# Keeping the first batch's embedding sums in DRAM for the second batch

## The chip, the cores and the metric

The kernel runs on one core of a Trainium2 chip. The metric is the device time of one execution in microseconds, the median of three runs. The profile is one more execution, taken by the hardware profiler.

The engines are named as in the profile: PE is the matrix engine (PEld its weight loads), DVE the vector engine, ACT the scalar engine, POOL the GpSimd engine, and SP the engine that issues most of the DMA transfers. A name with a q behind it (SPq, POOLq) is the engine's sequencer, which issues transfers.

## The reference

Two layers of attention work on a tensor of 2 batches, 512 channels and 64 x 32 = 2048 positions. The change concerns layer 0 alone. Its queries and keys are projections of the channels together with a position embedding of 64 rows, 32 of which depend on the row h of the position and 32 on its column w:

```python
emb = get_embeddings(B, H, W, FREQ_DIM, TIME_DIM, hidden_states.dtype)
qk_hs = jnp.concatenate([hidden_states, emb], axis=1)
qk_hs = qk_hs.reshape(B, -1, S).transpose(0, 2, 1)
q = qk_hs @ Wq
k = qk_hs @ Wk
v = v_hs @ Wv
...
scores = jnp.einsum('bhqd,bhkd->bhqk', q, k) * scale
attn = jax.nn.softmax(scores, axis=-1)
o = jnp.einsum('bhqk,bhkd->bhqd', attn, v)
...
return o + hidden_states
```

`get_embeddings` broadcasts the same embedding over the batches. The embedding's share of q and of k is thus the same for both batches. Layer 1 (a layer norm, Nystroem attention with landmarks, a residual and a feed-forward map) follows, and the change does not touch it.

## The kernel before, in words

All numbers are float32. Layer 0 goes through eight pairs of heads, four of batch 0 and then four of batch 1; pair (b, hp) is the two heads hp of batch b, 128 channels. The class `Heads0` (line 857) holds what a pair needs before its attention: q and k of 128 x 2048, and v. For q and for k this is

- the embedding's sum (`embedded`, lines 877 to 890). The embedding is kept as 64 rows by 64 + 32 columns, one column for each h and each w. A matmul (line 880) gives the projection of these 96 columns in a PSUM bank `fp`; DVE copies it to `ft` (line 882); POOL adds the part of h and the part of w, both broadcast, to `e`, 128 x 2048 (line 884). The pool `wpool0` has one buffer for each name, so `e` has one buffer, which q and k of all pairs share in turn;
- four projections, one for each block of 512 positions (lines 892 to 899): four matmuls into a PSUM bank `pp`, and a DVE add of the bank and the block of `e` into q or k.

The banks `fp`, `pp`, `vp`, `yp`, `mean`, `var` and `rs` all come from `bank()` (line 730), which has two buffers in turn.

The first pair does all this at the start of the kernel, with nothing beside it. SP issues the first loads there, about 7 MB, in this order: the first 128 columns of the query weights, the first block of x, the first 128 columns of the key weights, the other three blocks of x, the value weights, and the rest of the query and key weights.

Each further pair is prepared while the pair before it runs its attention. `attention0` (line 1045) goes through 4 blocks of queries (t) by 16 chunks of keys (c) in groups of two steps: the scores of two steps (PE, line 1057), the exps (ACT, line 1065), the sums of the exps (DVE, line 1075), and the values of the group before (PE, line 1087). After a group it may take units of work from a list of generators, the fillers. How many are due follows from a count: `due = n_filler * (i + GROUP) // len(steps)`, and `advance` takes up to three when two or more are due. A generator that yields `GAP` has nothing to do in this turn: the call goes on to the next generator, and the gap counts as no unit. `Heads0.N_UNITS` (line 860) is the count for one pair: 5 units for q, 5 for k, 4 for v and the bound.

The units of a pair are, for q: the embedding's matmul, copy and sum as a unit of its own, a gap, and four projections. Then the same for k, then four units of v. In pair (1,0) the order is another: its attention also has the residual projection and the norm of batch 0 as fillers (`finish0_units`, line 1017), and takes at least one unit after each group; the pair prepared there, (1,1), does k and v first, and q last, once the residual projection has used the q of batch 0 (`ready`, line 923). What is left of the units is done after the last group without attention beside it. In that stretch the norm's steps are (lines 971 to 1013): the sum over the four chunks of channels (DVE, 974 and 975), the mean (PE, 978), the difference (DVE, 979), the squares (ACT, 982 and 985) and their sum (DVE, 987 and 988), the variance (PE, 991), its root (ACT, 993), the reciprocal (DVE, 1008), the scaling (POOL 1010, DVE 1011), and the store of `xh` (POOL's queue, 1012). The block `xr` is loaded on SP's queue (1021).

After each block of queries, `sums` (line 1097) adds up the exps over the partitions (PE, `rs`), takes the reciprocal (DVE, 1102), spreads it by eight small transfers on SP's queue (`rinv`, line 789), and scales o on POOL (1105).

PE, DVE, ACT and POOL run their instructions in the order of the program. The order on SP's queue is set by a scheduler when the kernel is built: it puts a transfer as early as what it depends on allows by its own estimate. [...]

Of the kernel before, what the change touches and what calls it, by code (L numbers as in the profile page):

```python
# [10 lines left out]
F32 = mybir.dt.float32  # L11
# [5 lines left out]
P = 128  # L17
B, C, H, W = 2, 512, 64, 32
S = H * W
KC = C // P  # L20
HEADS, D = 8, 64
NPAIR = HEADS // 2
# [637 lines left out]
GAP = object()  # L660
# [3 lines left out]
def fast_path(  # L664
# [35 lines left out]
    nc = tc.nc  # L700
    dram = ctx.enter_context(tc.tile_pool(name="dram1", bufs=1, space=bass.MemoryType.DRAM))
# [12 lines left out]
    wpool0 = only0.enter_context(tc.tile_pool(name="w0", bufs=1))  # L714
# [3 lines left out]
    mT_d = dram.tile([P, KC, C], F32, name="mT_fd")  # L718
    k_d = dram.tile([B, NPAIR, P, S], F32, name="k_fd")
    X_d = dram.tile([B, NPAIR, 2, P, 2, LM], F32, name="X_fd")  # L720
    q_d = dram.tile([B, NPAIR, P, S], F32, name="q_fd")
    o_d = dram.tile([B, NPAIR, P, S], F32, name="o_fd")
    A_d = dram.tile([B, NPAIR, 2, P, 2, LM], F32, name="A_fd")
# [6 lines left out]
    def bank(name):  # L730
        return ps.tile([P, 512], F32, tag="pp", name=name)
# [60 lines left out]
    def advance(gens, n=1):  # L792


        made, i = 0, 0
        while made < n and i < len(gens):
            got = next(gens[i], gens)
            if got is gens:
                gens.pop(i)
            elif got is GAP:  # L800
                i += 1
            else:
                made += 1
        return made
# [5 lines left out]
    def gap(n=1):  # L810
        for _ in range(n):
            yield GAP
# [21 lines left out]
    def load_x(src, b, name, first=0, n=NTB):  # L834
        tiles = []
        for t in range(first, first + n):
            xb = block_of(xpool, "xb", f"{name}_{b}_{t}")
            nc.sync.dma_start(xb, chunked(src[b])[:, :, t * TB : (t + 1) * TB])
            tiles.append(xb)
        return tiles  # L840
# [16 lines left out]
    class Heads0:  # L857


        N_UNITS = 15  # L860

        def __init__(self, b, hp, xbs):
            self.b, self.hp, self.xbs = b, hp, xbs
            self.name = f"f0_{b}_{hp}"

        def begin(self):
            self.cols = slice(self.hp * P, (self.hp + 1) * P)
            self.k = kvpool.tile([P, S], F32, tag="k", name=f"k_{self.name}")
            self.v = kvpool.tile([P, NST, P], F32, tag="v", name=f"v_{self.name}")

        def embedded_and_projected(self, kind):

            cols, xbs = self.cols, self.xbs
            if kind == "q":
                self.q = qopool.tile([P, S], F32, tag="qo", name=f"q_{self.name}")

            def embedded(kind):

                fp = bank(f"fp_{kind}_{self.name}")
                nc.tensor.matmul(fp[:, : H + W], lhsT=we[kind][:, cols], rhs=emb_sb, start=True, stop=True)  # L880
                ft = wpool0.tile([P, H + W], F32, tag="ft", name=f"ft_{kind}_{self.name}")
                nc.vector.tensor_copy(ft, fp[:, : H + W])
                e = wpool0.tile([P, H, W], F32, tag="e", name=f"e_{kind}_{self.name}")
                nc.gpsimd.tensor_tensor(
                    e,
                    ft[:, :H].unsqueeze(2).to_broadcast([P, H, W]),
                    ft[:, H:].unsqueeze(1).to_broadcast([P, H, W]),
                    ALU.add,
                )
                return e.rearrange("p h w -> p (h w)")  # L890

            def project(kind, dst, e, t):
                toks = slice(t * TB, (t + 1) * TB)
                pp = bank(f"pp_{kind}_{self.name}_{t}")
                for k in range(KC):
                    nc.tensor.matmul(  # L896
                        pp, lhsT=w_sb[kind][:, k, cols], rhs=xbs[t][:, k, :], start=k == 0, stop=k == KC - 1
                    )
                nc.vector.tensor_tensor(dst[:, toks], pp, e[:, toks], ALU.add)  # L899

            dst = self.q if kind == "q" else self.k
            e = embedded(kind)
            yield
            yield GAP
            for t in range(NTB):
                project(kind, dst, e, t)
                yield
# [109 lines left out]
    def finish0_units(b, oTs, outs_done):  # L1017
        last = None
        for t in range(NTB):
            xb = block_of(lpool, "xr", f"xr_f0_{b}_{t}")  # L1020
            nc.sync.dma_start(xb, chunked(x[b])[:, :, t * TB : (t + 1) * TB])
            yield from gap()

            for m, _ in enumerate(out0_units(b, t, xb, oTs)):
                if last and m == 0:
                    next(last)
                yield
            if t == NTB - 1:
                outs_done.append(True)
            if last:  # L1030
                yield from gap()
            xn = block_of(lpool, "xn", f"xn_f0_{b}_{t}")
            last = norm0_steps(b, t, xb, xn, xn[:, :2, :])
            next(last)
            yield from gap(2)
            next(last)
            yield
            yield from gap(2)
            next(last)
            yield from gap(2)  # L1040
            next(last)
            yield
        next(last)
# [128 lines left out]
    def load_wo(w, name):  # L1172
        wo_sb = block_of(lpool, "wo", name)
        nc.sync.dma_start(wo_sb, chunked(w))
        return wo_sb
# [13 lines left out]
    def write_bands():  # L1189


        rows = block_of(lpool, "xn", "rows1").rearrange("p k n -> p (k n)")
        rows = rows[:, : HEADS * (BAND + 1)].rearrange("p (h q) -> p h q", h=HEADS)
        nc.vector.memset(rows, 0.0)
        nc.sync.dma_start(rows[:, :, :KER], convr.partition_broadcast(P))
        for h in range(HEADS):
            nc.sync.dma_start(band_d[h].rearrange("(p q) -> p q", q=BAND + 1), rows[:, h, :])
# [498 lines left out]
    oTs, finish, work = [], None, []  # L1696
    for n, (b, hp) in enumerate(todo[:-1]):
        nb, nhp = todo[n + 1]
        if nb != b:
            xbs = load_x(x, nb, "x0")  # L1700
        nxt = Heads0(nb, nhp, xbs)
        n_fill = Heads0.N_UNITS + 2 * len(work)
        if finish is None:
            units = nxt.units(wait=nb - b)
        else:

            units = nxt.units(False, lambda: outs_done)
            work.append(finish)
            n_fill += N_FINISH0
        work.append(units)  # L1710
        attention0(cur, work, n_fill, units, ffn_map if finish is None else None, finish is not None)
        finish = None
        oTs.append(cur.q)
        if n == 3:
            while ffn_map:
                advance(ffn_map)
            wo_sb = load_wo(wo0, "wo_f0")
            write_bands()
        if hp == NPAIR - 1:
            outs_done = []  # L1720
            finish = finish0_units(b, oTs, outs_done)
            oTs = []
        cur = nxt
# [45 lines left out]
    b = B - 1  # L1769
# [300 lines left out]
@with_exitstack  # L2070
def conv_attn_hybrid(
    ctx: ExitStack,
    tc: tile.TileContext,
    x: bass.AP,
    emb: bass.AP,
    freq: bass.AP,
    time: bass.AP,
    wq0: bass.AP,
    wk0: bass.AP,
    wv0: bass.AP,  # L2080
    wo0: bass.AP,
    b0: bass.AP,
    *rest: bass.AP,
):

    nc = tc.nc
    keep = ctx.enter_context(tc.tile_pool(name="keep_f", bufs=1))
    bad = keep.tile([P, 1], F32, name="bad")
    bad_i = keep.tile([P, 1], I32, name="bad_i")
    in_order = {mybir.EngineType.PE, mybir.EngineType.DVE, mybir.EngineType.Activation, mybir.EngineType.Pool}  # L2090
    with tc.manual_schedule(engines=in_order):
        fast_path(tc, x, freq, time, wq0, wk0, wv0, wo0, b0, *rest, bad)
    nc.vector.tensor_copy(bad_i, bad)
    again = nc.values_load(bad_i[:1, :1])
    with tc.If(again > 0):
        general_path(tc, x, emb, wq0, wk0, wv0, wo0, b0, *rest)
# [59 lines left out]
```

## Time and profile before

| | |
|---|---|
| median of three runs | 2775.44 us (2773.93 to 2777.14) |
| profiled execution | 2775.64 us |
| its span in the profile | 2773.8 us |
| mean granted PE clock | 0.993 |
| layer 0's attention ends at about | 1330 us |
| DMA in the whole span | 157.22 MB, mean 57 GB/s |
| L884, POOL sum `e` (16) | 3.6 to 4.6 us each |
| L882, DVE copy `ft` (16) | 0.25 us each |
| L880, PE matmul `fp` (32, two for each sum) | 0.31 us each |

The three rows of L880, L882 and L884 are the work on the embedding's sums, for both batches. A line of the timeline has the start in us, the busy time in us, the engine, the line of the kernel, the operation, and output and inputs; at the end, in brackets, is the idle time of the engine before it and what ended that. Runs of the same instruction are merged, with their count after an x. In the rows by slices, each digit is the busy share of one fortieth of the span in tenths.

### The profile page before, as it was taken

What the parts mean: (1) busy time and instruction counts of PE and PEld (TensorE: products, weight loads), DVE (VectorE), ACT (ScalarE), POOL (GpSimd) and SP (SyncE); (2) the same over time, 40 slices, a digit from 0 to 9 for tenths busy, and PEclk for the clock granted to TensorE, in tenths of its full rate; (3) what the DMA queues carried; (4) which work ended last, traced back from release to release, by engine and by line L of the source; (5) the groups of instructions that cost most, each with busy time, mean ns of one, the idle gap of its engine ahead of it and who ended that gap; (6) DMA issues with size and microseconds to landing.
All of it is one profiled execution on the core that took longest, in us unless ns stands there. A gap on an engine that the chain in (4) does not pass through costs nothing. (4 is left out here: it accounts for less than half of the span.)

```text
span 2773.8 us, 41257 instructions
## 1 busy us (share of the span) xinstructions
PE 2712.4 (98%) x17010; PEld 1365.7 (49%) x17010; DVE 1638.7 (59%) x2076; ACT 905.8 (33%) x1352; POOL 197.2 (7%) x133
## 2 busy tenths in 40 slices
PE   9999999999999999999999999999999999999898
PEld 5343443434343334343344455777677766555334
DVE  3768787774557765747657444544644545556455
ACT  1344343433335244435412223233332323221210
POOL 1101101010001200100002000000000000000000
PEclk9999999999999999999999999999999999999999
DMA  3000000201111200012025532313111202111301
GB/s 115 12 9 9 13 6 7 69 24 50 32 50 54 80 9 7 8 49 64 24 87 186 201 118 92 97 34 115 54 36 58 81 9 90 38 66 31 106 32 47
DMA packets 110358, 157.22 MB, mean 57 GB/s; under 512 B 16065, under 2 KB 67793, under 8 KB 107601
## 3 DMA queue, kind: packets, MB, share of 16 engines
q1 hardware_dynamic: 105664, 137.68, 15.7%
q0 software_dynamic: 4416, 16.79, 1.6%
q8 instruction: 135, 2.21, 0.4%
q14 instruction: 63, 0.51, 0.1%
q10 hardware_dynamic: 80, 0.03, 0.0%
HBM read 82.48 MB, written 55.19 MB: 50 GB/s over the span
## 5 line engine op out<-in xcount | busy, mean ns | idle before, releaser
L1075 DVE TENSOR_TENSOR acc_f<-acc_f,p_f 128x1024 f32<-128x1024 f32 x448 | 589.4, 1316 | 235.6 <-ACT p_f L1065 207.0
L1065 ACT ACTIVATE p_f<-sc_f 128x1024 f32<-128x1024 f32 x512 | 496.4, 1021 | 561.9 <-PE sc_f L1057 550.4
L1057 PE MATMUL sc_f<-q_f,k_f 64*64 64x512 f32 x4096 | 491.7, 595 | 2.4 <-ACT p_f L1065 2.4
L1087 PE MATMUL av_f<-p_f,v_f 64*64 64x512 f32 x4096 | 484.3, 589 | 0.0
L1087 PEld LDWEIGHTS av_f<-p_f,v_f 64*64 64x64 f32 x4096 | 156.5, 133 | 283.0 <-issue 283.0
L1057 PEld LDWEIGHTS sc_f<-q_f,k_f 64*64 64x64 f32 x4096 | 144.8, 133 | 280.9 <-issue 256.0
L1230 PE MATMUL pp<-xh,w 128*128 128x512 f32 x512 | 233.0, 608 | 0.7 <-ACT q L1233 0.7
L1230 PEld LDWEIGHTS pp<-xh,w 128*128 128x128 f32 x512 | 96.5, 194 | 123.2 <-issue 116.0
L1523 PE MATMUL pb<-R 128*128 128x192 f32 (+1 forms) x640 | 151.4, 383 | 1.6 <-DVE M L1536 1.6
L1523 PE MATMUL pa<-M 128*128 128x192 f32 (+1 forms) x640 | 150.6, 380 | 0.0
L941 PEld LDWEIGHTS vp_f<-wv_f,x 128*128 128x128 f32 x1024 | 115.6, 192 | 12.7 <-issue 11.0
L941 PE MATMUL vp<-w,xh 128*128 128x128 f32 x1024 | 120.8, 276 | 0.0
L941 PEld LDWEIGHTS vp<-w,xh 128*128 128x128 f32 x1024 | 117.0, 192 | 7.2 <-issue 4.2
L1523 PEld LDWEIGHTS pb<-R 128*128 128x128 f32 x640 | 107.8, 192 | 25.2 <-DVE M L1536 2.3
L896 PE MATMUL pp_q_f<-x,wq_f 128*128 128x512 f32 x256 | 115.9, 606 | 2.9 <-DMA x<-in_x_dram 1.5
L941 PE MATMUL vp_f<-wv_f,x 128*128 128x128 f32 x1024 | 118.5, 276 | 0.0
L1523 PEld LDWEIGHTS pa<-M 128*128 128x128 f32 x640 | 108.0, 193 | 21.0 <-ACT M L1514 2.5
L956 PE MATMUL yp_g<-o,wo_f 128*128 128x512 f32 x256 | 115.5, 598 | 0.8 <-DVE y_g L1662 0.8
L956 PE MATMUL yp_f<-q_f,wo_f 128*128 128x512 f32 x256 | 114.0, 598 | 2.2 <-issue 1.2
L1673 PE MATMUL fp_g<-xn_g,mT 128*128 128x512 f32 (+1 forms) x264 | 115.7, 589 | 0.0
L896 PE MATMUL pp_k_f<-x,wk_f 128*128 128x512 f32 x256 | 114.1, 599 | 0.4 <-DVE q_f L899 0.4
L1105 POOL TENSOR_TENSOR q_f<-q_f,rinv_f 128x512 f32<-128x512 f32 x32 | 45.9, 1434 | 920.4 <-DMA rinv_f<-acc_f 920.4
(196 smaller groups left out, 2762.0 us busy)
## 6 DMA issues: line engine op xcount, KB each, us to landing
xh<-xh_fd SPq DMA_DIRECT2D x12, 1024.0 KB, 5.4
rinv_f<-acc_f SPq DMA_DIRECT2D x256, 32.0 KB, 1.9
xr_f<-in_x_dram SPq DMA_DIRECT2D x8, 1024.0 KB, 5.2
x_fd<-xr_f POOLq DMA_DIRECT2D x8, 1024.0 KB, 4.6
xh_fd<-xn_f POOLq DMA_DIRECT2D x8, 1024.0 KB, 4.6
k_fd<-k SPq DMA_DIRECT2D x32, 256.0 KB, 2.8
q_fd<-q SPq DMA_DIRECT2D x32, 256.0 KB, 2.9
xb_g<-x_fd SPq DMA_DIRECT2D x32, 256.0 KB, 4.3
```

Source lines behind the costliest of these rows:

```text
L896: nc.tensor.matmul(pp, lhsT=w_sb[kind][:, k, cols], rhs=xbs[t][:, k, :], start=k == 0, stop=k == KC - 1)
L941: nc.tensor.matmul(vp[:, j * P : (j + 1) * P], lhsT=xb[:, k, j * P : (j + 1) * P], rhs=w_of(k), start=k == 0, stop=k == KC - 1,)
L956: nc.tensor.matmul(yp, lhsT=wo_sb[:, k, m * P : (m + 1) * P], rhs=oTs[k][:, toks], start=k == 0, stop=k == NPAIR - 1,)
L1057: nc.tensor.matmul(sc[r * D : (r + 1) * D, h, :], lhsT=hd.k[rows, lo : lo + D], rhs=hd.q[rows, t * TB : (t + 1) * TB], start=True, stop=True,)
L1065: nc.scalar.activation(p, sc, AF.Exp, scale=D**-0.5)
L1075: nc.vector.tensor_tensor(acc, first if c == 1 else acc, p, ALU.add)
L1087: nc.tensor.matmul(av[r][half, :], lhsT=hd.v[keys, c, half], rhs=pp[keys, h, :], start=c == 0, stop=c == NST - 1,)
L1105: nc.gpsimd.tensor_tensor(o, o, rinv, ALU.mult)
L1230: nc.tensor.matmul(pp, lhsT=self.w[j][:, c, :], rhs=xhs[t][:, c, :], start=c == 0, stop=c == KC - 1)
L1523: nc.tensor.matmul(dst, lhsT=lhsT[:, k, t * P : (t + 1) * P], rhs=rhs[:, k, :], start=k == 0, stop=k == 1)
L1673: nc.tensor.matmul(fp[:, cols], lhsT=mT[:, k, m * P : (m + 1) * P], rhs=self.xn[:, k, cols], start=k == 0, stop=k == KC - 1,)
```

## The change

Pairs of batch 0 compute the embedding's sums as before, and store each of them, 1 MB, to a new tensor `e_fd` in DRAM, on SP's queue. Pairs of batch 1 compute none: they load the sum into the same buffer `e`, on SP's queue too. In a pair of batch 1 the embedding is no unit any more; two gaps stand in its place, and the count of units is 13 where it was 15.

```diff
+    e_d = dram.tile([2, NPAIR, P, S], F32, name="e_fd")
...
-        N_UNITS = 15
-
         def __init__(self, b, hp, xbs):
             self.b, self.hp, self.xbs = b, hp, xbs
             self.name = f"f0_{b}_{hp}"
+            self.n_units = 13 if b else 15
...
             def embedded(kind):
+                e = wpool0.tile([P, H, W], F32, tag="e", name=f"e_{kind}_{self.name}")
+                flat, kept = e.rearrange("p h w -> p (h w)"), e_d["qk".index(kind), self.hp]
+                if self.b:
+                    nc.sync.dma_start(flat, kept)
+                    return flat
                 fp = bank(f"fp_{kind}_{self.name}")
                 nc.tensor.matmul(fp[:, : H + W], lhsT=we[kind][:, cols], rhs=emb_sb, start=True, stop=True)
                 ft = wpool0.tile([P, H + W], F32, tag="ft", name=f"ft_{kind}_{self.name}")
                 nc.vector.tensor_copy(ft, fp[:, : H + W])
-                e = wpool0.tile([P, H, W], F32, tag="e", name=f"e_{kind}_{self.name}")
                 nc.gpsimd.tensor_tensor(
                     e,
                     ft[:, :H].unsqueeze(2).to_broadcast([P, H, W]),
                     ft[:, H:].unsqueeze(1).to_broadcast([P, H, W]),
                     ALU.add,
                 )
-                return e.rearrange("p h w -> p (h w)")
+                nc.sync.dma_start(kept, flat)
+                return flat
...
             e = embedded(kind)
-            yield
-            yield GAP
+            if self.b:
+                yield from gap(2)
+            else:
+                yield
+                yield GAP
...
-        n_fill = Heads0.N_UNITS + 2 * len(work)
+        n_fill = nxt.n_units + 2 * len(work)
```

## The prediction

> **What bounds the kernel now.** I read the page first, then the list of what the TensorE waits for over the attention stages, then the timeline at the three places where it does wait, and the granted clock there.
>
> ```profile
> PE 2712.4 (98%) x17010; PEld 1365.7 (49%) x17010; DVE 1638.7 (59%) x2076; ACT 905.8 (33%) x1352; POOL 197.2 (7%) x133
> PE   9999999999999999999999999999999999999898
> DMA  3000000201111200012025532313111202111301
> ```
>
> The PE is busy in every slice; the DMA engines and POOL are nearly idle in the first 1330 us, which hold layer 0 (the stage that the change edits). So what counts is (a) PE instructions that go and (b) PE waits that come or go. The waits of the PE between 640 and 1320 us (engine, line, releaser: total us, times, longest):
>
> ```profile
> PE mean_n L978 <- DVE xn_f L975: 2.8, 1, 2.8
> PE var_n L991 <- DVE xr_f L988: 1.6, 1, 1.6
> PE sc_f L1057 <- ACT p_f L1065: 1.3, 3, 0.7
> PE yp_f L956 <- issue: 1.2, 1, 1.2
> ```
>
> All but the sc_f row lie in pair (1,0), the one that runs beside batch 0's residual and norm. No row there names the embedding's sum: in batch 1 no consumer waits for `e`. The removed POOL adds are off the path. At the kernel's start it is otherwise:
>
> ```profile
> 18.91 0.43 SPq L1132 DMA_DIRECT2D sc_f<-in_scales_dram  x1
> 25.30 0.25 DVE L882 COPY ft_k_f<-fp_k_f 128x96 f32<-128x96 f32 x1
> 25.44 14.00 PE L896 MATMUL pp_k_f<-x,wk_f 128*128 128x512 f32 x32 [0.40 <-DVE q_f L899]
> 25.70 3.63 POOL L884 TENSOR_TENSOR e_k_f<-ft_k_f 128x2048 f32<-128x2048 f32 x1 [8.96 <-DVE ft_k_f L882]
> 29.36 0.69 DVE L899 TENSOR_TENSOR k_f<-pp_k_f,e_k_f 128x512 f32<-128x512 f32 x1 [3.81 <-POOL e_k_f L884]
> ```
>
> The first k add waits for the POOL sum; the PE runs on without a gap only because two PSUM banks last until 25.44 + 2 x 3.43 = 32.3 us. The end of pair (1,0):
>
> ```profile
> 901.72 1.13 PE L991 MATMUL var_n<-xr_f,mean_w 128*128 128x512 f32 x2 [1.64 <-DVE xr_f L988]
> 917.78 0.46 PE L880 MATMUL fp_q_f<-emb_f,weq_f 64*128 64x96 f32 x2
> 919.71 3.65 POOL L884 TENSOR_TENSOR e_q_f<-ft_q_f 128x2048 f32<-128x2048 f32 x1
> 920.68 3.77 DVE L974 TENSOR_TENSOR xn_f<-xr_f 128x1024 f32<-128x1024 f32 x1 [1.88 <-DMA xh_fd<-xn_f]
> 925.23 1.19 PE L978 MATMUL mean_n<-xn_f,mean_w 128*128 128x512 f32 x2 [2.83 <-DVE xn_f L975]
> 926.21 12.14 PE L896 MATMUL pp_q_f<-x,wq_f 128*128 128x512 f32 x24
> ```
>
> Here the DVE add takes 3.77 us beside the POOL sum and 1.22 us without it (the same line at 832.79). The stage view shows a granted clock of 0.54 and 0.61 in 926-930 us, right after the 2.83 us wait: the 24 matmuls take 12.14 us, where 24/32 of the 14.00 us above is 10.5.
>
> **What the Trainium skill says.** "TensorE: Matmul & The Clock Gate", Part 1 (what's actually happening): an idle window of about 3.4 us drops the array to half clock, and a busy one brings it back; the windows run freely. The trace agrees: half clock for some 3.5 us after waits of 2.02, 2.83, 3.24 and 3.47 us, none after 1.24 or 1.5. "GPSIMD Engine Reference", Specifications: its SBUF interface is shared with VectorE instructions that have two SBUF inputs; 3.77 against 1.22 us agrees. "DMA: Bandwidth & Descriptors", Queues, rings and completion order: each DMA engine takes the descriptors of one ring in order, so a store issued behind loads moves behind them. The trace agrees: the 16 KB load issued at 18.91 lands 8.8 us later, a 32 KB one elsewhere in 1.9.
>
> **The change, part by part.**
>
> *1. Eight L880 pairs of matmuls go (PE).* One costs what the group around it grows by: score-to-score start is 3.43 us without one (62.87 to 66.31) and 3.93 with one (66.31 to 70.24), so 0.49 us. Seven of them: 3.4 us gained; the eighth (q of pair (1,1)) is counted in 5. The eight L882 copies (0.25 us) and L884 sums (3.6 to 4.6 us) are hidden behind a PE that is full: nothing. One rs wait of 0.46 us at 610.2, on a DVE slowed by the sum just before, should go: 0.5 gained.
>
> *2. Eight stores of 1 MB from batch 0 (SP queue).* Beside attention they cost nothing: DMA share there is 0.03 and the tile's next writer comes 46 us or more later. The first is different: it is issued at about 18.9 us (the place of sc_f, after e_q ended at 16.74) behind the initial loads, and `e` has one buffer, so the k sum now waits for its landing. DMA runs full until about 26.6 us; without the 256 KB of qidx, which now comes later, until some 25.9. Then 1 MB at 320 to 380 GB/s (rate of 14-21 us) is 2.8 to 3.3 us, and 0.5 to 1.3 for the receipt: landing at 29.3 to 31. Taken 30.2. Then 3.63 POOL, 0.7 DVE: the third k projection starts at 34.6 and not 32.3. Loss 2.3 us (1.6 to 3.1). Such a wait may also drop the clock, 1.7 us; at even odds or a little less, 0.8.
>
> *3. Eight loads of 1 MB in batch 1.* Each waits for the last reader of the one `e` buffer, and SP's rinv transfers stand behind it. In the built order each is placed before a rinv whose sums come later than that reader, so nothing behind is held up. The tightest is e_k of pair (1,0): its buffer is free after the last q add, and between this and the first k add lie a mp unit (3.6), three groups (3.43 each) and the first k unit: some 17 us for a load that takes about 5 (xr_f, 5.2). The e_q of pair (1,1) is loaded long before its use. Nothing; if that cover were gone, see the third rival.
>
> *4. Units counted 13 and not 15, two gaps: the fillers shift by up to two groups.* The PE works through the same list, so a shift costs only where it makes a wait. At the start of pair (1,0) two yp units now stand in the first group. The second needs the bank of the last rs, free after DVE's reciprocal at 712.7 (before, yp waited 1.24 us for the same). Now: scores end at 707.4, first yp unit at 710.9, wait 1.9: loss 0.65; at 1.9 us the clock may drop too, 0.5 on average. Bounds 0 to 2.4.
>
> *5. The end of pair (1,0).* The third block's mean comes one group earlier, ahead of its variance by three groups in place of two; in the new order the squares stand ahead of the last two exps on ACT. So the 1.64 us wait goes. From that var_n the chain is as before: xr landing 6.4 us later, reciprocal 3.34, POOL 3.38, store of xh landing at +18.96 after var; then the DVE add at 1.22 and 0.7 to the mean at +20.95 (before +23.51). The PE is there at about +19.4, so a wait of 1.5 us stays, too short by the trace for half clock. Then 0.98 and three q units of 3.43: the fourth block's var_n at +32.3, before +36.47. Gain 1.6 + 4.2 = 5.8 us. If the clock still drops, 4.1; if the first wait stays as well, 2.5; at most 6.3.
>
> *Sum.* Gained 3.4 + 0.5 + 5.8 = 9.7; lost 2.3 + 0.8 + 0.65 + 0.5 = 4.25: 5.4 us less. From the profiled execution (2775.64 us, span 2773.8) that is 2770.2; the median, 2775.44, is 0.2 below it: 2770.0 us.
>
> **The rivals.**
> - *The start costs more.* Landing at 31, both waits with half clock: 3.1 + 1.7 + 0.65 + 1.7 = 7.2 in place of 4.25: 2773 us. For it: the queue is full and its end is blurred. Against: waits of about 2 us are at the edge.
> - *The end of (1,0) gives nothing*, as another chain (xr's load, the store of xh) takes the place of both waits: 3.9 + 0.5 - 4.25, about zero: 2775.3 us. For it: that chain is serial over five engines and queues. Against: each of its links stands in the timeline and ends 2.5 us sooner.
> - *Slower: the loads of e_k come late.* One buffer means that e_k can't be fetched before q is done. If the landing comes later than about 17 + 3.4 us after the last reader (SP held by an earlier transfer, or 1 MB loads ahead), the PE fills its two banks and stops, in pairs (1,0), (1,2) and (1,3). At 3 us each with half clock after it, 3 x 4.7 = 14 us: 2784 us. For it: x (4 MB) and xr go through the same queue. Against: they are issued at other times, and DMA share is 0.03 to 0.2.
>
> **How the numbers follow.** The forecast has 0.62, the dear start 0.15, the empty end 0.13, the late loads 0.10. The forecast's own range, from the bounds of parts 2, 4 and 5, is 2766.5 to 2773; with two of the rivals in it, 2766.5 to 2777. A change of 0.2% is 5.5 us, about what a measurement tells from none, and the forecast of 5.4 stands on this edge: six tenths of its chance count as faster, 0.38, as the DVE's relief from the POOL sums, costed at nothing in part 1, can only add; 0.02 more come from the rivals. Within 0.2%: 0.46. Slower, with what is left of the late loads and the dear start: 0.14.
>
> **What would show it.** Right: PE wait at the third k projection of 1.6 to 3.1 us at about 32 us, with the k sum started at about 30; no L880 after the first batch's; no wait at the third block's var_n, a DVE add of 1.2 us and no 0.5 clock near 920-930 us. Wrong: k or q adds of batch 1 that wait for a DMA of e, rinv issues held behind such a load, or a POOL start later than 31 us.

## The result, and the profile after

The changed kernel takes 2765.56 us (median of 8 runs, 2763.73 to 2768.42), the kernel before 2774.51 us (8 runs beside it, 2773.41 to 2777.14). The ratio is 0.9969, with a 95% interval of 0.9959 to 0.9978: 6 to 11 us faster, where 5.4 were forecast and 2766.5 was the lower end of the range. The medians differ by 9.0 us. The profiled execution of the changed kernel (2763.73 us, span 2761.9) is the fastest of its eight, and that of the kernel before (2775.64 us) lies 1.1 us above its median, so the distance of the two profiles, 11.9 us, is larger than that of the medians.

Lines in the changed kernel stand one to nine further down than before (L880 is L886, L896 is L902, L956 is L965, L978 is L987, L991 is L1000, L1057 is L1066). From the page of the changed kernel: busy time, and the slices of the PE and of its clock.

```profile
PE 2703.8 (98%) x16994; PEld 1363.3 (49%) x16994; DVE 1629.0 (59%) x2068; ACT 905.8 (33%) x1352; POOL 164.7 (6%) x125
PE   9999999999999999999999999999999999899898
PEclk9999999999999999999999999999999999999999
```

Sixteen matmuls and eight POOL sums are gone, as the diff says. PE busy time fell by 8.6 us, and more than half of that is not the matmuls that went: the profile of before has three more stretches of 3.4 us at half clock than this one, which is some 5 us of longer matmuls. Waits don't count as busy at all. What the PE waited for in the changed kernel at the start (0 to 60 us, first row) and from 640 to 1320 us (the others); columns are total us, times, longest:

```profile
PE pp_k_f L902 <- DVE k_f L905: 1.3, 1, 1.3
...
PE sc_f L1066 <- ACT p_f L1074: 1.6, 4, 0.7
PE mean_n L987 <- DVE xn_f L984: 1.4, 1, 1.4
PE yp_f L965 <- DVE xr_f L972: 0.9, 1, 0.9
```

Of the three waits of pair (1,0) that the prediction shows, the mean's is halved, the variance's is gone, and the 1.2 us of `yp` under "issue" are gone too, which the prediction had not seen coming. (The `yp` row that is left, for `xr`, stood at 1.0 us before.) The start, in the timeline:

```profile
18.72 0.35 SPq L895 DMA_DIRECT2D e_fd<-e_q_f  x1
29.21 3.63 POOL L889 TENSOR_TENSOR e_k_f<-ft_k_f 128x2048 f32<-128x2048 f32 x1 [12.75 <-DMA e_fd<-e_q_f]
33.62 7.13 PE L902 MATMUL pp_k_f<-x,wk_f 128*128 128x512 f32 x16 [1.33 <-DVE k_f L905]
```

The k sum does wait for the first store, as forecast, but it starts at 29.21 and not at 30.2, and the PE's wait of 1.33 us brings no half clock: the 16 matmuls behind it take 7.13 us. The end of pair (1,0):

```profile
898.71 1.12 PE L1000 MATMUL var_n<-xr_f,mean_w 128*128 128x512 f32 x2
917.54 1.23 DVE L983 TENSOR_TENSOR xn_f<-xr_f 128x1024 f32<-128x1024 f32 x1 [2.04 <-DMA xh_fd<-xn_f]
919.55 1.12 PE L987 MATMUL mean_n<-xn_f,mean_w 128*128 128x512 f32 x2 [1.40 <-DVE xn_f L984]
920.51 10.46 PE L902 MATMUL pp_q_f<-x,wq_f 128*128 128x512 f32 x24
930.81 1.02 PE L1000 MATMUL var_n<-xr_f,mean_w 128*128 128x512 f32 x2
```

The last of these lines in the kernel before:

```profile
938.19 1.02 PE L991 MATMUL var_n<-xr_f,mean_w 128*128 128x512 f32 x2
```

No wait at the first var_n, a DVE add of 1.23 us in place of 3.77, a mean wait of 1.40, and 24 matmuls at full clock in 10.46 us in place of 12.14. Variance to variance it is 32.10 us, where it was 36.47 (901.72 to 938.19).

To see where the time went, the start of every row-sum matmul (`rs`, four per pair) is compared between two timelines. What one pair adds to the difference to the kernel before, in us, worked out from those starts (pairs as they run; the pair that runs also carries the projections of the next one):

| stage, up to its last rs in the timeline before | changed kernel |
|---|---|
| start, to 91 us | +1.31 |
| pairs (0,0) to (0,2), to 531 us | 0.00 |
| pair (0,3), to 705 us | -0.97 |
| pair (1,0), to 939 us | -7.72 |
| pair (1,1), to 1098 us | -1.59 |
| pair (1,2), to 1257 us | -1.59 |
| pair (1,3), to 1399 us | 0.00 |
| sum | -10.56 |

Behind 1399 us, where layer 0's attention ends in the timeline before (and not at 1330 us), no instruction is changed. The distance of the two traces still moves there, to 12.3 us at 1438 us, where the profile of before has a stretch of half clock that the other lacks, and it ends at 11.9. Single executions of the changed kernel alone lie up to 4.7 us apart. So the table says where the two traces part, and the medians say how much the change is worth.

### The profile page after: what moved, and what is told of

Same layout as the page of the kernel before. It is cut to its first block, busy times and chain, and to the rows that moved or that the text cites. A ratio compares the mean times of both kernels' runs of the same rounds, so it can differ in the third digit from the quotient of the medians.

```text
span 2761.9 us, 41236 instructions
## 1 busy us (share of the span) xinstructions
PE 2703.8 (98%) x16994; PEld 1363.3 (49%) x16994; DVE 1629.0 (59%) x2068; ACT 905.8 (33%) x1352; POOL 164.7 (6%) x125
## 5 line engine op out<-in xcount | busy, mean ns | idle before, releaser
L1084 DVE TENSOR_TENSOR acc_f<-acc_f,p_f 128x1024 f32<-128x1024 f32 x448 | 582.6, 1300 | 208.8 <-ACT p_f L1074 180.2
L1066 PE MATMUL sc_f<-q_f,k_f 64*64 64x512 f32 x4096 | 491.1, 594 | 2.7 <-ACT p_f L1074 2.7
L1066 PEld LDWEIGHTS sc_f<-q_f,k_f 64*64 64x64 f32 x4096 | 145.8, 133 | 285.6 <-issue 262.0
L902 PE MATMUL pp_q_f<-x,wq_f 128*128 128x512 f32 x256 | 114.4, 599 | 2.1 <-DVE q_f L905 1.4
L965 PE MATMUL yp_g<-o,wo_f 128*128 128x512 f32 x256 | 115.5, 598 | 0.8 <-DVE y_g L1671 0.8
L902 PE MATMUL pp_k_f<-x,wk_f 128*128 128x512 f32 x256 | 114.3, 599 | 1.7 <-DVE k_f L905 1.3
L965 PE MATMUL yp_f<-q_f,wo_f 128*128 128x512 f32 x256 | 113.7, 598 | 0.9 <-DVE xr_f L972 0.9
```

The costliest lines, as they stand in the source:

```text
L902: nc.tensor.matmul(pp, lhsT=w_sb[kind][:, k, cols], rhs=xbs[t][:, k, :], start=k == 0, stop=k == KC - 1)
L965: nc.tensor.matmul(yp, lhsT=wo_sb[:, k, m * P : (m + 1) * P], rhs=oTs[k][:, toks], start=k == 0, stop=k == NPAIR - 1,)
L1066: nc.tensor.matmul(sc[r * D : (r + 1) * D, h, :], lhsT=hd.k[rows, lo : lo + D], rhs=hd.q[rows, t * TB : (t + 1) * TB], start=True, stop=True,)
L1084: nc.vector.tensor_tensor(acc, first if c == 1 else acc, p, ALU.add)
```

## The experiments

The kernel before was run again beside each group of experiments: 2773.87 us (37 runs) beside the shift alone, the load alone, the first sum aside and the one sum; 2774.25 (44 runs) beside the first store twice, the pairs kept, the POOL sum kept and the one store; 2773.52 (17 runs) beside the shift in both batches and the factors kept. All ratios are to it. Each kernel has one trace, so differences between traces below about 1 us at the start, and everything behind 1399 us, can be the launch and not the edit.

**The shift alone, and the load alone.** The first kernel computes the sums in both batches, and keeps only the count of 13 and the two gaps:

```diff
-                if self.b:
-                    nc.sync.dma_start(flat, kept)
-                    return flat
...
-                nc.sync.dma_start(kept, flat)
```

> Only the turns of batch 1's units change (13 counted, two gaps); no store, no load, all 16 sums computed as before. Theory A (the ledger read from the two profiles: a shift saves some 0.3 us for each turn that is merged with another, and the 1.64 us wait of the third block's var_n goes; fp, the POOL sum beside the norm, the 2.8 us mean wait and the half clock stay): 3 to 5 us faster than before, and from var_n of block 3 to var_n of block 4 about 36.5 us as before. Theory B (the prediction's part 4: a shift is free except where it makes or takes a wait): 1.6 to 2.9 us faster, nothing in pairs (1,1) and (1,2).

Measured: 2776.56 us (2774.05 to 2779.12), ratio 1.0008 [1.0000, 1.0017]. Neither theory: the shift alone is slower, by 2.7 us in the medians, though the interval just touches 1. By the rs starts, pair (0,3) loses 4.5 us and pair (1,0) gains 2.1, of which 1.64 is the wait at var_n; the pairs (1,1) and (1,2) gain 0.5 each, which is theory A's part. The loss in (0,3), POOL and DVE lines of its timeline, then the PE's:

```profile
559.34 3.68 POOL L885 TENSOR_TENSOR e_q_f<-ft_q_f 128x2048 f32<-128x2048 f32 x1 [11.30 <-DVE ft_q_f L884]
559.57 4.00 DVE L1156 TENSOR_TENSOR wl_f<-wl_f,hits_f 128x512 f32<-128x512 f32 x1
569.67 1.28 DVE L900 TENSOR_TENSOR q_f<-pp_q_f,e_q_f 128x512 f32<-128x512 f32 x2
570.41 5.36 PE L897 MATMUL pp_q_f<-x,wq_f 128*128 128x512 f32 x8 [3.43 <-DVE q_f L900]
```

The same place in the changed kernel:

```profile
560.89 0.69 DVE L1161 TENSOR_TENSOR wl_f<-wl_f,hits_f 128x512 f32<-128x512 f32 x1
566.62 1.28 DVE L905 TENSOR_TENSOR q_f<-pp_q_f,e_q_f 128x512 f32<-128x512 f32 x2
567.36 3.70 PE L902 MATMUL pp_q_f<-x,wq_f 128*128 128x512 f32 x8 [0.51 <-DVE q_f L905]
```

With the shift, three q projections stand in one turn, and two PSUM banks hold two of them. The third waits until the DVE has added the first. Beside the POOL sum a DVE operation of 0.69 us takes 4.00, everything behind it in the DVE's queue is 3 us later, and the PE waits 3.43 us and then runs at half clock (eight matmuls in 5.36 us, not 3.70). Without the sum the wait is 0.51.

The second kernel keeps store and load, with the old count of 15 and one unit and one gap:

```diff
-            self.n_units = 13 if b else 15
+            self.n_units = 15
...
-            if self.b:
-                yield from gap(2)
-            else:
-                yield
-                yield GAP
+            yield
+            yield GAP
```

> Stores and loads as in the change, but 15 counted and a unit and a gap as before, so that every other unit stands where it stood. Theory A: start 1.3 us later, eight fp less (0.49 each, 3.9), one rs wait less (0.5), the stretch from var_n to var_n 4.4 us shorter (0.5 of it the fp), var_n's wait of 1.64 us stays: 6.5 to 7.5 us faster than before in the profile; in pairs (1,1) and (1,2) 1.0 us each and not 1.6. Theory B: 5 to 8 us, and the same 1.6 us in these pairs, since the fp would then cost 0.8.

Measured: 2766.79 us (2765.24 to 2771.07), ratio 0.9976 [0.9965, 0.9986]: most of the gain. The pairs (1,1) and (1,2) save 1.3 us each, between the theories' 1.0 and 1.6, and the profiled execution is 8.8 us below that of before, over A's 7.5. By the rs starts it becomes 10.24 us shorter from the start's end to 1399 us, the changed kernel 11.87, and the shift alone 1.40 longer. So the shift is worth -1.6 us where the sums are loaded and +1.4 where POOL makes them. (The medians of the load alone and the changed kernel differ by 1.2 us, inside their intervals.) With the load, the shift saves 2.0 us in pair (1,0) and 0.3 in each of (1,1) and (1,2), and costs 1.0 in (0,3).

**Is it the POOL sum or the matmul pair?** One sum of POOL is put back, that of q of pair (1,1), which stands beside the mean's wait:

```diff
-                if self.b:
+                if self.b and (self.b, self.hp, kind) != (1, 1, "q"):
...
-                nc.sync.dma_start(kept, flat)
+                if not self.b:
+                    nc.sync.dma_start(kept, flat)
```

> The change, with one sum of batch 1, q of pair (1,1), computed as before in place of its load. Theory A (the POOL sum slows the DVE add in front of the mean, the longer wait drops the clock): DVE add at 3.7 us and not 1.2, mean wait 2.5 to 3, half clock for 3.5 us after it, var_n to var_n 36.5 us: 4.4 us slower than the change. Rival (the mean's wait is set by the store of xh and the fp alone counts): 0.5 to 1 us slower, no half clock.

Measured: 2768.93 us (2764.91 to 2771.15), ratio 0.9981 [0.9974, 0.9988], 3.4 us above the changed kernel's median, which was measured apart. Its timeline:

```profile
917.27 3.64 POOL L889 TENSOR_TENSOR e_q_f<-ft_q_f 128x2048 f32<-128x2048 f32 x1
918.24 3.76 DVE L984 TENSOR_TENSOR xn_f<-xr_f 128x1024 f32<-128x1024 f32 x1 [1.88 <-DMA xh_fd<-xn_f]
922.79 1.12 PE L988 MATMUL mean_n<-xn_f,mean_w 128*128 128x512 f32 x2 [2.83 <-DVE xn_f L985]
923.75 10.46 PE L903 MATMUL pp_q_f<-x,wq_f 128*128 128x512 f32 x24
```

The DVE add of 3.76 us and the mean wait of 2.83 are back with the one sum, as theory A has it. In this execution no half clock follows (10.46 us), where in the kernel before it followed on the same wait; without it the loss to the changed kernel is 2.5 us by the rs starts, and not 4.4. This edit puts back the matmul pair of that sum too.

Then the two were taken apart. The changed kernel with the matmul pairs kept beside the loads, their result unused:

```diff
                 if self.b:
+                    fp = bank(f"fp_{kind}_{self.name}")
+                    nc.tensor.matmul(fp[:, : H + W], lhsT=we[kind][:, cols], rhs=emb_sb, start=True, stop=True)
+                    ft = wpool0.tile([P, H + W], F32, tag="ft", name=f"ft_{kind}_{self.name}")
+                    nc.vector.tensor_copy(ft, fp[:, : H + W])
                     nc.sync.dma_start(flat, kept)
```

> The changed kernel, with the eight fp matmul pairs of batch 1 and their copies kept (their result is not used). A (an fp pair costs the PE 0.49 us, and the turns it splits 0.1-0.3 more): 3.9-6 us over the changed kernel, 2769.5-2771.5, with no mean_n wait above 1.5 us and no long pp_q wait in (0,3). B (the gain of the load is relief of the DVE from the POOL sums and the fp pairs lie beside other work): within 1.5 us of the changed kernel, 2765-2767.

Measured: 2768.95 us (2766.02 to 2772.53), ratio 0.9980 [0.9974, 0.9986]. The total lies between the theories, and A's marks are there: no pp_q wait in (0,3), and the mean waits less than in the changed kernel, not longer:

```profile
PE yp_f L969 <- issue: 1.2, 1, 1.2
...
PE mean_n L991 <- DVE xn_f L988: 0.3, 1, 0.3
```

By the rs starts it is 3.94 us behind the changed kernel over batch 1's projections, a mean of 0.49 for each of the eight matmul pairs. They are not alike: the two that run beside the attention of (0,3) cost 0.5 together, the two beside (1,0) 1.2, the two beside (1,1) and the two beside (1,2) 1.1.

The other half is the POOL sum without the pair. In a first kernel POOL adds factors copied from x (so the values of batch 1 are others):

```diff
                 if self.b:
-                    nc.sync.dma_start(flat, kept)
+                    ft = wpool0.tile([P, H + W], F32, tag="ft", name=f"ft_{kind}_{self.name}")
+                    nc.vector.tensor_copy(ft, xbs[0][:, 0, : H + W])
+                    nc.gpsimd.tensor_tensor(
+                        e,
...
+                    )
                     return flat
```

> The changed kernel with no fp pair in batch 1 and no load either: POOL still makes a sum of the same size into e, from a copy of 96 columns of x (so the values of batch 1 differ from the reference's). A (the POOL sum slows the DVE's adds, which makes the long pp_q wait in pair (0,3) and the 2.8 us mean_n wait in (1,0)): both waits come back, some 3.4+1.7+1.4 to 3.4+1.7+3.1 us, so 2772-2773.5, near the shift alone less eight fp pairs. B (those waits come from the fp pair, its copy and its bank, not from the POOL sum): within 1.5 us of the changed kernel.

Measured: 8549.54 us. The total says nothing of the edit: with these values the later stages do more work (45378 matmuls in its profile, 16994 in the changed kernel's). Its layer 0 can be read, and it shows both waits of theory A: 3.9 us at pp_q in pair (0,3), 3.9 at the mean. A second kernel has the right values: it keeps the sum's two factors, 48 KB, in DRAM, and POOL adds them in both batches:

```diff
-    e_d = dram.tile([2, NPAIR, P, S], F32, name="e_fd")
+    e_d = dram.tile([2, NPAIR, P, H + W], F32, name="e_fd")
...
                 if self.b:
-                    nc.sync.dma_start(flat, kept)
-                    return flat
...
+                    nc.sync.dma_start(ft, kept)
```

> The changed kernel with the two factors of the sum (128x96 numbers, 48 KB) kept in DRAM in place of the sum: no fp pair in batch 1, but the POOL sum stays; values as the reference's. A (fp pairs are worth 3.9 us of the load's gain and the POOL sums 9): the pp_q wait of 3-4 us in (0,3) with its half clock and the mean_n wait of 2.8-3.9 us in (1,0) are there; layer 0 ends 2-3.5 us before that of the kernel before, 2770.5-2773. B (the POOL sums are off the path, as the prediction's part 1 priced them): within 1.5 us of the changed kernel.

Measured: 2774.16 us (2770.34 to 2779.55), ratio 1.0000 [0.9991, 1.0008]. It is no different from the kernel before. The waits are as A has them; the total is 1.2 us over A's upper end, while its profiled execution (2771.15 us, of 2770.34 to 2779.55) lies inside. Waits of the PE in this kernel, 60 to 640 us and 640 to 1320 us:

```profile
PE pp_q_f L902 <- DVE q_f L905: 3.8, 1, 3.8
...
PE mean_n L987 <- DVE xn_f L984: 3.9, 1, 3.9
```

The four kernels with the shifted order form a square. What each adds to the difference to the kernel before, from the end of the start to 1399 us, by the rs starts:

| | POOL sums in batch 1 | no POOL sums |
|---|---|---|
| matmul pairs in batch 1 | +1.40 (shift alone) | -7.93 (pairs kept) |
| no matmul pairs | -1.94 (factors kept) | -11.87 (changed kernel) |

So the pairs are worth 3.3 to 3.9 us in this order, and the POOL sums 9.3 to 9.9. By stage the 9.3 are 5.0 in (0,3) and 4.3 in (1,0), and nothing elsewhere. In (0,3) the factors' kernel has two windows of half clock (3.41 us) and the shift alone one (1.71).

**The start.** The first q sum goes into a tile of its own, so that the k sum needn't wait for its store:

```diff
+                if self.name == "f0_0_0" and kind == "q":
+                    e = block_of(lpool, "wo", "e_q_first").rearrange("p k n -> p (k n)").rearrange("p (h w) -> p h w", w=W)
```

> The change, with the first q sum of all in another free buffer, so that the k sum does not wait for its store. Theory A (the start's loss is this wait alone): the third k projection follows without a wait, the first scores come 1.3 us earlier than in the change, and this stays to the end: 1.3 us faster than the change, 10 against before. Rival (the queue behind the initial loads holds something else too, as the weights of the second pair): less than 0.5 us.

Measured: 2766.27 us (2763.74 to 2770.09), ratio 0.9969 [0.9957, 0.9981]: no different from the changed kernel. The wait at the third k projection is gone from its trace, but its profiled execution waits 1.98 us for a q add earlier and runs at a clock of 0.66 from 18 to 23 us. The start varies by such things from launch to launch: at the first rs, kernels with no large store there stand at +0.91 (shift alone) and -0.27 us (factors kept) against before. Whether this kernel gains anything stays open.

The first store issued twice, the second to another place:

```diff
                 nc.sync.dma_start(kept, flat)
+                if self.name == "f0_0_0" and kind == "q":
+                    nc.sync.dma_start(e2_d, flat)
```

> The changed kernel, with the very first store (q sum of pair 0) written a second time to another place. A (the start is priced by the landing of that store: the k sum starts when it has landed): one more 1 MB store at 320-380 GB/s puts the landing 2.8-3.3 us later, the PE wait at the third k projection grows from 1.33 to 4.1-4.6 us and drops the clock once (1.7 us): 4-5 us over the changed kernel, 2769.5-2771. B (the start does not hang on the store; what differs there is the launch): same as the changed kernel, wait about 1.3 us.

Measured: 2770.62 us (2765.78 to 2775.37), ratio 0.9989 [0.9983, 0.9996], 5 us above the changed kernel. Theory A fits in total and place, with a wait a little under its 4.1 us. Its timeline, and its clock by stretch (from:to, length, then busy time of PE, PEld, DVE, ACT and POOL, each with its count, clock, DMA share, GB/s):

```profile
31.27 3.63 POOL L890 TENSOR_TENSOR e_k_f<-ft_k_f 128x2048 f32<-128x2048 f32 x1 [15.17 <-DMA e_fd<-e_q_f]
35.68 4.54 PE L905 MATMUL pp_k_f<-x,wk_f 128*128 128x512 f32 x6 [3.75 <-DVE k_f L908]
```

```profile
36.00:40.00 4.00, 4.00 (x6) 1.54 (x5) 0.22 (x1) 0.00 (x0) 0.00 (x0) 0.57 0.55 229
40.00:44.00 4.00, 4.00 (x11) 1.79 (x10) 0.69 (x1) 0.00 (x0) 0.00 (x0) 1.00 0.00 0
```

The k sum is 2.06 us later than in the changed kernel, and 2.5 later counted from the issue of the first store (18.26 and 18.72). Inside this one trace the second store lands 2.9 us after the first. The PE waits 3.75 us, and 3.4 us at half clock follow.

All stores but one left out, all loads reading that one:

```diff
-                flat, kept = e.rearrange("p h w -> p (h w)"), e_d["qk".index(kind), self.hp]
+                flat, kept = e.rearrange("p h w -> p (h w)"), e_d[1, 2]
...
-                nc.sync.dma_start(kept, flat)
+                if kind == "k" and self.hp == 2:
+                    nc.sync.dma_start(kept, flat)
```

> The changed kernel with seven of its eight stores left out; all eight loads read the one sum that is still stored, the k sum of pair 2 (so batch 1 adds another sum than the reference's). A (only the first store costs, 1.3 us at the third k projection, the rest lie beside attention): that wait goes, 0.5-1.5 us under the changed kernel, 2764-2765.5, everything after 60 us alike. B (the stores beside attention cost as well, through the queue or through e's release): 3 us or more under it.

Measured: 2764.58 us (2762.72 to 2767.66), ratio 0.9966 [0.9954, 0.9978]. Theory A: 1 us below the changed kernel's median, inside the scatter; in the traces 0.6 us at the start, and behind it all rs starts of layer 0 move together. The stores beside attention cost nothing.

**The shift in both batches.** The count of 13 and the two gaps for batch 0 as well:

```diff
-            self.n_units = 13 if b else 15
+            self.n_units = 13
...
-            if self.b:
-                yield from gap(2)
-            else:
-                yield
-                yield GAP
+            yield from gap(2)
```

> The changed kernel with the count of 13 and two gaps in batch 0 as well. A (the shift pays 0.25 us wherever it puts a group's row sums directly behind a turn of 128-row matmuls, twice per pair): three pairs of batch 0 have 0.5 us less each, 1.5 us under the changed kernel, 2763.5-2765.5, no new wait. B (beside a POOL sum the shift costs, as it did alone in pair (0,3), because q's projections come before the DVE is ready to add): a pp_q wait of 1-4 us in one or more of the pairs (0,0) to (0,2), 2766-2775.

Measured: 2763.14 us (2761.01 to 2763.90), ratio 0.9960 [0.9946, 0.9973]: the fastest of all kernels here, 2.4 us below the changed kernel's median, though the intervals overlap. By the rs starts, pairs (0,0) to (0,2) take 4.14 us less, and not 1.5. Two things add up. The first is the turn that A speaks of. In the timeline before, in pair (1,1), the row sums and the k projections are two turns between 64-row matmuls:

```profile
1012.08 1.90 PE L1087 MATMUL av_f<-p_f,v_f 64*64 64x512 f32 x16
1014.09 0.64 PE L778 MATMUL rs_f<-acc_f,ones 128*32 128x256 f32 x8
1014.65 1.95 PE L1057 MATMUL sc_f<-q_f,k_f 64*64 64x512 f32 x16
1016.42 1.90 PE L1087 MATMUL av_f<-p_f,v_f 64*64 64x512 f32 x16
1018.25 7.13 PE L896 MATMUL pp_k_f<-x,wk_f 128*128 128x512 f32 x16
1025.31 1.95 PE L1057 MATMUL sc_f<-q_f,k_f 64*64 64x512 f32 x16
```

In the changed kernel they are one:

```profile
1003.61 1.90 PE L1096 MATMUL av_f<-p_f,v_f 64*64 64x512 f32 x16
1005.44 7.13 PE L902 MATMUL pp_k_f<-x,wk_f 128*128 128x512 f32 x16
1012.50 0.64 PE L779 MATMUL rs_f<-acc_f,ones 128*32 128x256 f32 x8
1013.07 1.95 PE L1066 MATMUL sc_f<-q_f,k_f 64*64 64x512 f32 x16
1014.84 1.90 PE L1096 MATMUL av_f<-p_f,v_f 64*64 64x512 f32 x16
1016.55 1.90 PE L1066 MATMUL sc_f<-q_f,k_f 64*64 64x512 f32 x16
```

From a group of values to the next scores: 2.57 + 8.89 us before, 9.46 + 1.71 after, 0.29 less. It happens twice in a pair (k and v), and the shift alone shows it bare: -0.50 and -0.49 us in pairs (1,1) and (1,2); with the load it is -0.3 in each. The second thing is a wait. In the changed kernel the rs of batch 0 stand three times behind a DVE that is late with its adds after a POOL sum, this one after the sum of 283.26 us:

```profile
PE rs_f L779 <- DVE acc_f L1084: 3.0, 3, 1.2
...
285.83 1.90 PE L1096 MATMUL av_f<-p_f,v_f 64*64 64x512 f32 x16
288.91 0.64 PE L779 MATMUL rs_f<-acc_f,ones 128*32 128x256 f32 x8 [1.19 <-DVE acc_f L1084]
```

With the k projections ahead of the rs, the PE has 7 us of work while the DVE catches up, and this row of the waits is gone from the trace. Together that would be 1.5 + 3.0 us, near the 4.14. The long pp_q wait of theory B did not come in batch 0.

## Why the prediction was wrong

The direction and the largest term were right, but the sum was too small: 5.4 us were forecast, and 9.0 came in the medians. Another 0.9 us of the distance between 2770.0 and 2765.56 is the base: the median of three runs, 2775.44, stood above that of the eight. The prediction's own terms, put in the stages in which they fall, beside the two traces (us, minus is faster):

| stage | forecast | terms | traces |
|---|---|---|---|
| start | +3.1 | first store 2.3, clock 0.8 | +1.31 |
| (0,3) | -1.4 | two matmul pairs, the rs wait | -0.97 |
| (1,0) | -5.1 | one pair, the `yp` wait +1.15, the end -5.8 | -7.72 |
| (1,1) and (1,2) | -2.0 | two pairs in each | -3.18 |
| sum | -5.4 | | -10.56 |

Step by step:

1. *Matmul pairs, 0.49 us each*: 3.94 / 8 = 0.49 in the mean, but that this is the forecast's figure is in part luck. The matmul pairs beside the attention of (1,1) and (1,2) cost 0.54 each. The k pair in the first group of (1,0) costs next to nothing itself, as the scores behind it then wait 0.28 us for the exps; the q pair at the end of (1,0) costs nothing either, as the mean waits 0.28 us with it and 1.40 without. But the k pair takes a PSUM bank, and that is why `yp` waited, which this part doesn't count: the wait of 1.24 us is there in both kernels that have batch 1's matmul pairs in the shifted order (shift alone, pairs kept), and gone in the two that have none (load alone, factors kept). From the timelines of the changed kernel with the pairs kept, and of the changed kernel itself:

```profile
709.94 0.46 PE L884 MATMUL fp_k_f<-emb_f,wek_f 64*128 64x96 f32 x2
715.25 7.11 PE L969 MATMUL yp_f<-q_f,wo_f 128*128 128x512 f32 x16 [1.24 <-issue]
```

```profile
709.98 1.90 PE L1096 MATMUL av_f<-p_f,v_f 64*64 64x512 f32 x16
711.81 7.13 PE L965 MATMUL yp_f<-q_f,wo_f 128*128 128x512 f32 x16
```

The rs wait of 0.46 us, which part 1 also counts, went, but it is gone in the shift alone too, where all sums are kept, so the sum beside it was not needed for that. That the sums cost nothing outside part 5 does not hold in the shifted order, where the stall in (0,3) is theirs; the change itself never meets it. No kernel here takes the sums away in the old order and keeps the pairs, so what they cost there is not shown.

2. *The first store, 2.3 us and 0.8 for the clock*: the wait is there, at the place named, but 1.33 us long and with no half clock. The mis-sized term is the landing: the store landed at 29.05 us and the k sum started at 29.21, not 30.2. One more store measured 2.1 to 2.9 us, by how it is counted, so the 2.8 to 3.3 us taken for 1 MB are rather long, and the 0.5 to 1.3 us added for a receipt stand on no line. That the clock did not drop is chance as much as the shorter wait (see the last section).
3. *The loads, nothing*: right. No add of batch 1 waits for a DMA of `e`. The loads take 4.8 us (median); the tightest, e_k of (1,0), is issued at 593.5 us and first used at 610.7. Every first rinv transfer of a block is issued within 0.06 us of its reciprocal, so no load held it up. The third rival falls.
4. *The shift, "costs only where it makes a wait"*: the step that failed. The two `yp` units were put in the first group of (1,0). They stand after the second, behind its values: 711.81 us, not 707.4. The first takes the bank that no matmul pair holds any more, and the second the bank of the last rs, free since the reciprocal ended at 713.0, 2.4 us before it is needed. So there is no wait where 1.9 us were forecast. From the rs of 705 us to the first `yp` it is 6.46 us, where it was 7.77: 1.3 us gained, where this part and the k pair together had 0.66 lost. The sentence is wrong the other way too: a shift also pays, with no wait on either side, where it puts a short 128-row operation beside a long one; the shift alone gains 0.5 us so in each of (1,1) and (1,2), and about 0.4 of the gain in (1,0) may be the same. What the shift made was a wait of 0.51 us at pp_q in (0,3), which was not priced.
5. *The end of (1,0), 5.8 us*: measured 1.64 + (36.47 - 32.10) = 6.0. The mean wait is 1.40 (1.5 forecast). Right; and the pairs kept (0.3 us) and the factors kept (3.9 us) show that it is the POOL sum which made the long one. The 1.64 us at var_n are the shift's: they are gone in the shift alone and still there in the load alone.

Of the 5.1 us between the sums, 2.0 are at `yp`, 1.8 at the start, and most of the rest the turns in (1,1), (1,2) and (1,0), less the 0.5 in (0,3). The two remaining rivals fall as well: the start costs less than the forecast, not more, and the end of (1,0) gives all it should.

## What to carry to other kernels

Price a removed operation by everything that it holds besides its engine: here the PSUM bank of a small matmul (1.24 us) and the DVE's time under a POOL instruction (9.3 to 9.9 us) were worth more than the matmuls themselves (2.7 us, the bank's wait apart). A reordering is free to test alone, and should be: this one loses 1.4 us in the traces without the load and pays 1.6 with it, so its value can't be added up from the two edits taken apart. Where units are moved, write out the new list of turns to the end of the first few groups before pricing a wait, and put short 128-row matmuls next to long ones.

## What was not expected of the hardware

*A POOL add of this kernel does not slow the DVE's two-input operations beside it, it stops them.* In the shift alone the sum ends at 559.34 + 3.68 = 563.02 us; the DVE operation that began beside it ends at 563.57, 0.55 later, and takes 0.69 alone. With the one sum restored, the sum ends at 920.91, the add at 922.00, 1.09 later; alone it takes 1.23. It goes the other way as well: in the timeline before, the second of these lines starts after the first DVE add has begun,

```profile
72.61 5.80 DVE L1075 TENSOR_TENSOR acc_f<-acc_f,p_f 128x1024 f32<-128x1024 f32 x2
72.81 4.51 POOL L884 TENSOR_TENSOR e_q_f<-ft_q_f 128x2048 f32<-128x2048 f32 x1 [43.48 <-DVE ft_q_f L882]
```

and the sum takes 4.51 us where others take 3.65: 0.9 us more, about the 1.0 us that the first add (1.23) still had to run. The second add then ends at 78.41, 1.09 after the sum. The Trainium skill ("GPSIMD Engine Reference", Specifications) speaks of contention between the two; by these times the one that comes second waits for nearly all that is left of the other's instruction.

*Whether a wait drops the clock depends on where it falls.* In the kernel before, half clock begins at 926.15, 1434.74, 1506.42 and 1543.97 us. The distances are 149, 21 and 11 times 3.413 us, and each of these drops lasts 3.41 us: the changes lie on a grid of 3.41 us, in every trace here, and its place differs from one execution to the next. The wait of 2.83 us before the mean has 2.5 us in one step of this grid in the kernel before, and half clock follows; with one sum restored an edge at 921.45 us (counted back from that trace's first drop, at 1494.89) cuts it into 1.5 and 1.3, and none follows. At the start, 1.98 us inside one step dropped the clock (first sum aside), 1.99 cut in two halves did not (shift alone), nor did 1.72 inside one step (load alone). So for the waits read here in layer 0 the limit lies between 1.72 and 1.98 us of one step; the prediction quoted an idle window of about 3.4 us and took these shorter waits as agreeing with it. It is no full rule: at 1434.74 us the clock drops after a step in which the PE was idle for only 0.7 us. One drop costs 1.7 us (16 matmuls in 8.83 us and not 7.13, first sum aside), and it moves single executions by that step, also in stages that an edit doesn't touch.
